# Three edits in a two-layer kernel: norm sums on ScalarE, the first chunk's delta on VectorE, all result rows fetched at once

## The chip, the cores and the metric

The kernel runs on one core of a Trainium2 chip. A core has a tensor engine for matmuls (PE, with its weight loads shown as PEld), a vector engine (DVE, VectorE), an activation engine (ACT, ScalarE), a general engine (POOL, GpSimd), and a sync engine (SP) that here only issues transfers. Each engine works through its own list of instructions in order; an instruction can wait on semaphores for another engine or for a transfer (DMA). SBUF is the on-chip memory with 128 partitions, PSUM the memory that matmuls write to.

The metric is the device time in microseconds (us) of one execution; less is better. The profile is of one further execution, and its own time is given beside the median of the runs.

## The reference

The input is x, 64 sequences of 64 tokens with 256 features (4096 tokens), and a condition for each sequence. Two layers each add an attention-like part and a feed-forward part to x:

```python
x = x + attn0(cond_scan0(x, cond))          # softmax attention over a conditioned scan
x = x + ffn0(modulated(x, cond))            # the 1.58-bit feed-forward below
x = x + mamba(rnn(x, cond))                 # selective scan over a tanh recurrence
x = x + moe_ffn(mixture(x, cond))           # two mixtures of experts, top 2 of 8 each
```

The parts that the change touches, cut to their core:

```python
def bitlinear(x, norm_w, w):                # ffn0: w1 (1024 x 256), then w2 (256 x 1024)
    v = mean(x**2, axis=-1)
    x_norm = x * rsqrt(v + 1e-8) * norm_w
    scale = 127 / clip(max(abs(x_norm)), 1e-5)
    x_q = clip(round(x_norm * scale), -128, 127) / scale
    return x_q @ ternary(w).T
h = bitlinear(x, n1, w1); h = act_scale * relu(h)**2 + act_bias; y = bitlinear(h, n2, w2)

delta = softplus(delta_lr @ W_dt + b_dt)    # mamba, 512 inner features, 16 states
dA = exp(delta[..., None] * A); dBx = delta[..., None] * B * xc[..., None]
h = dA_t * h + dBx_t; y = sum_n(h * C_t) + D * x_t          # along each sequence

x = x + sum over a token's 2 chosen experts of  weight * expert(x)      # the last step
```

## The kernel before

Activations are held with features on the partitions: 256 features are two blocks (KD = 2) of 128, and the 4096 tokens are worked in 8 chunks of 512 (NCH = 8, CH = 512). The program is written in a framework that takes tiles from pools, sets the semaphores, and orders each engine's instructions itself from what depends on what; where a written line lands in an engine's list therefore depends on its neighbours too. The stages follow each other: conditioned scan and attention (to about 377 us of the profile), ffn0 with the recurrence of layer 1 beside it (to about 656), mamba with the shared experts of the mixture beside it (to about 1895), the routed experts of the mixture, the experts of the last feed-forward (to about 2745), and the last rows.

**ffn0.** Tokens are worked in 16 pairs of 128 rows. Each of 23 turns runs nine stages, each on a different pair, so that seven pairs are in flight; from the eighth turn on the turns also issue four steps of the recurrence (L820 on PE, L829 on ACT). In each turn:

- ACT squares and sums the rows of one pair's first input (L596 on gm, 256 features) and of another pair's hidden layer (L596 on h, 1024 features), into a small tile `ss`.
- `roots_of` turns both sums into 1/sqrt(mean + eps): L605 on DVE makes mean + eps for each of the two, L608 on DVE a first guess from the bits, and L610 to L620 on POOL eleven small operations of refinement.
- `weighted` multiplies by the norm's weights and takes the largest magnitude: for gm with L632 on POOL, for h with L634 on DVE; L635 on DVE is the maximum.
- `rounded` makes the scale (L643, L644 on DVE, L645, L646 on POOL; L644 reads what L620 wrote) and rounds (L651 on ACT for h, L653 on DVE for gm, L655 on DVE for both).
- The rest are products, with L660 on POOL for the scaled input, L669, L697 and L725 on DVE, and L695, L712, L721 on ACT.

**mamba.** Each chunk has two halves (PI = 2 of the NI = 4 blocks of 128 inner features) of 16 states: 32 steps a chunk, 256 in all. `head` makes a chunk's convolution, its delta and delta times x. Its last lines for each half make softplus by L963 to L969 on ACT and L967 on DVE and end with three operations of 128x1024 elements on POOL:

```python
nc.gpsimd.tensor_add(z, z, t2)      # L970
nc.gpsimd.tensor_sub(z, z, u)       # L971
nc.gpsimd.tensor_mul(u, z, v.xc[:, i0 : i0 + PI, :])    # L972
```

Chunk 0's head runs whole ahead of the loop; the others are spread over the steps of the chunk before. A step has L1045 on POOL (input, two steps ahead, into one of five `hb` buffers), L1052 on ACT (decay, one step ahead), L1084 on DVE (two scans), L1086 on DVE (times C, spread by PE at L997), and L1100 on PE (sum of states). The scans and products of all steps are kept in order by an order token.

**Last rows.** The last experts scatter their weighted rows to DRAM (`ffn_y`, two rows a token), by L1352 on POOL. x, stored in DRAM as x_mid by the mamba stage, is loaded in eight pieces of 512 KB by L2010, between the last expert tiles of the feed-forward; expert weights (L1537) and gathered rows (L1345) are loaded through the same SP queue. For each chunk, `routing.fetch` (L1361) then brings 1024 KB of rows into one of two buffers, PE transposes the blocks of 128x128 and adds a token's two results in PSUM (L2022, 16 matmuls a chunk), DVE adds x (L2031), and SP sends 256 KB for each k (L2032). The buffers come from the same pool `px` as the pieces of x.

Of the kernel before, what the change touches and what calls it, by code (L numbers as in the profile page):

```python
# [13 lines left out]
F32 = mybir.dt.float32  # L14
BF16 = mybir.dt.bfloat16
I32 = mybir.dt.int32
AF = mybir.ActivationFunctionType
ALU = mybir.AluOpType
# [3 lines left out]
P = 128  # L22
B, L, D = 64, 64, 256
NT = B * L
CH = 512
NCH = NT // CH
KD = D // P
# [10 lines left out]
def setup(ctx, tc, a):  # L38

    nc = tc.nc  # L40
    g = SimpleNamespace(nc=nc, tc=tc, a=a)
    const = ctx.enter_context(tc.tile_pool(name="const", bufs=1))
    g.ident = const.tile([P, P], F32, name="ident")
    make_identity(nc, g.ident)
    g.identb = const.tile([P, P], BF16, name="identb")
    make_identity(nc, g.identb)
    g.ones = const.tile([P, 1], F32, name="one")
    nc.vector.memset(g.ones, 1.0)
    g.magic = const.tile([P, 1], F32, name="magic")
    nc.vector.memset(g.magic, MAGIC)  # L50
    g.eps = const.tile([P, 2], F32, name="eps")
    nc.vector.memset(g.eps, EPS)
    g.guess = const.tile([P, 4], F32, name="guess")
    nc.vector.memset(g.guess, 1597463007.0)
    g.condT = const.tile([P, KD, B], F32, name="condT")
    nc.sync.dma_start(g.condT, a["condT"].rearrange("(k p) b -> p k b", p=P))
    g.x = tc.dram_tile((D, NT), F32, name="x_mid").rearrange("(k p) t -> p k t", p=P)
    return g
# [24 lines left out]
def bank(g, shape=(P, CH), dt=F32, tag="ps"):  # L83
    tag = g.tag or tag
    return g.psum.tile(list(shape), dt, tag=tag, name=tag)
# [485 lines left out]
def ffn0(g, w, steps, loads):  # L571
# [5 lines left out]
    nc, tc = g.nc, g.tc  # L577
# [7 lines left out]
    with (  # L585
# [12 lines left out]
        def roots_of(turn_, which):  # L598


            st = roots[turn_] = p3.tile([P, 4, 2, T], F32, name="roots")
            v, r, y, u = (st[:, i, which, :] for i in range(4))
            ss = sums.pop(turn_)
            for i, n in ((0, D), (1, F))[which]:
                nc.vector.scalar_tensor_tensor(st[:, 0, i, :], ss[:, i, :], 1.0 / n, g.eps, ALU.mult, ALU.add)  # L605
            flat = lambda t: t.rearrange("p i t -> p (i t)")
            first = g.guess[:, : flat(v).shape[1]]
            nc.vector.scalar_tensor_tensor(flat(r).bitcast(I32), flat(v).bitcast(I32), -0.5, first, ALU.mult, ALU.add)  # L608
            gp = nc.gpsimd
            gp.tensor_mul(y, r, r)  # L610
            gp.tensor_mul(y, y, v)
            gp.tensor_scalar(u, y, 0.375, -1.25, ALU.mult, ALU.add)
            gp.tensor_mul(u, u, y)
            gp.tensor_scalar(u, u, 1.875, None, ALU.add)
            gp.tensor_mul(r, r, u)
            gp.tensor_mul(y, r, r)
            gp.tensor_mul(y, y, v)
            gp.tensor_scalar(y, y, -0.5, 1.5, ALU.mult, ALU.add)
            gp.tensor_mul(r, r, y)
            gp.tensor_scalar(u, r, 127.0 / 1e-5, None, ALU.mult)  # L620
# [109 lines left out]
        for turn_ in range(NP + depth):  # L730
# [6 lines left out]
            for i, (stage, late) in enumerate(stages):  # L737
                if i % 2 == 0:
                    next(more, None)
                p = turn_ - late  # L740
# [120 lines left out]
def mamba(g, w, hs, beside):  # L861
# [3 lines left out]
    nc, tc = g.nc, g.tc  # L865
# [5 lines left out]
    PI = 2  # L871
# [6 lines left out]
    with (  # L878
# [17 lines left out]
        rows = 2 * 32 + S  # L896
# [12 lines left out]
        def head(c, v):  # L909

            tok = ts(c, CH)
            v.xc = p2.tile([P, NI, CH], F32, name="xc")
            v.delta, v.dx, v.sz = [], [], []
            v.dbc = p2.tile([W, CH], F32, name="dbc")
            v.parts = parts[c % 2]
            for i in range(NI):
                ps = one()
                for k in range(KD):
                    nc.tensor.matmul(ps, w.Win[:, k, ts(i, P)], hs2[:, k, tok], start=(k == 0), stop=(k == KD - 1))  # L919
                    if k == 0:  # L920
                        yield MID
                acc = v.xc[:, i, :]
                nc.scalar.activation(acc, ps, AF.Identity, bias=w.col[:, 0, i : i + 1], scale=w.taps[:, i, 3:4])
                for s in range(1, 4):
                    to = seq(acc)[:, :, s:]
                    nc.vector.scalar_tensor_tensor(  # L926
                        to, seq(ps)[:, :, : L - s], w.taps[:, i, 3 - s : 4 - s], to, ALU.mult, ALU.add
                    )
                yield
            nc.scalar.activation(v.xc, v.xc, AF.Silu)  # L930
            yield
            ps = one()
            for i in range(NI):
                nc.tensor.matmul(ps[:W, :], w.Wxp[:, i, :], v.xc[:, i, :], start=(i == 0), stop=(i == NI - 1))
                if i < NI - 1:
                    yield MID
            nc.scalar.copy(v.dbc, ps[:W, :])

            v.B = tc.dram_tile((S, CH), F32, name=f"B{c}")
            nc.sync.dma_start(v.B, v.dbc[R : R + S, :])  # L940


            r = slice(C0, W)
            nc.scalar.copy(v.parts[32 : 32 + S, :], ps[r, :])
            nc.vector.tensor_sub(ps[r, :], ps[r, :], v.parts[32 : 32 + S, :])
            nc.scalar.copy(v.parts[0:S, :], ps[r, :])
            nc.vector.tensor_sub(v.parts[64 : 64 + S, :], ps[r, :], v.parts[0:S, :])
            yield


            for i0 in range(0, NI, PI):
                z, u = (p3.tile([P, PI, CH], F32, name=n) for n in ("delta", "dx"))
                v.delta.append(z)
                v.dx.append(u)
                t2 = p1.tile([P, PI, CH], F32, name="t2")
                for i in range(PI):
                    ps = one()
                    nc.tensor.matmul(ps, w.Wdt[:, ts(i0 + i, P)], v.dbc[:R, :], start=True, stop=True)
                    nc.scalar.activation(z[:, i, :], ps, AF.Relu, bias=w.col[:, 1, i0 + i : i0 + i + 1])
                    nc.scalar.activation(u[:, i, :], ps, AF.Abs, bias=w.col[:, 1, i0 + i : i0 + i + 1])  # L960
                    yield
                nc.scalar.activation(u, u, AF.Exp, scale=-1.0)
                nc.scalar.activation(t2, u, AF.Identity, bias=unit[:, 0:1])  # L963
                for i in range(PI):
                    ps = one()
                    nc.scalar.activation(ps, t2[:, i, :], AF.Identity, bias=unit[:, 1:2])
                    nc.vector.tensor_sub(u[:, i, :], ps, u[:, i, :])  # L967
                    yield
                nc.scalar.activation(t2, t2, AF.Ln)  # L969
                nc.gpsimd.tensor_add(z, z, t2)  # L970
                nc.gpsimd.tensor_sub(z, z, u)  # L971
                nc.gpsimd.tensor_mul(u, z, v.xc[:, i0 : i0 + PI, :])  # L972
                yield

        def gates(c, v, i0):
# [94 lines left out]
        for s in range(LAST):  # L1070
            c, j = divmod(s, STEPS)
            p, n = divmod(j, S)
# [25 lines left out]
            for i in range(PI):  # L1098
                for t in range(CH // P):
# [4 lines left out]
                        start=(n == 0 and t == 0),  # L1104
                        stop=(n == S - 1 and t == CH // P - 1),
                        is_transpose=True,
                        skip_group_check=True,
# [8 lines left out]
            while left < (j + 1) * LEFT // (STEPS - AHEAD):  # L1116
                left += 1
                got = next(pieces, None) if mid else next(urgent, END)
                if got is END:
                    got = next(pieces, None)  # L1120
# [12 lines left out]
TT = CH // P  # L1133
# [777 lines left out]
def mixtures(g, mix, x, weights, out, last, work, close):  # L1911
# [6 lines left out]
    nc, tc = g.nc, g.tc  # L1918
# [13 lines left out]
    with ExitStack() as ctx:  # L1932
# [5 lines left out]
        n = moe0.ntl  # L1938
# [67 lines left out]
        xs = []  # L2006
# [3 lines left out]
            nc.sync.dma_start(x, g.x[:, :, ts(c, CH)])  # L2010
            xs.append(x)
        some(tiles2, None)
        for c in range(NCH):
            rows = px.tile([P, TT, 2, D], F32, name=f"rows3_{c % 2}")
            routing.fetch(c, rows)
            x = xs[c]
            for k in range(KD):
                po = bank(g, tag="acc")

                for t in range(TT):  # L2020
                    for j in range(2):
                        nc.tensor.matmul(  # L2022
                            po[:, ts(t, P)],
                            rows[:, t, j, ts(k, P)],
                            g.ident,
                            start=(t == 0 and j == 0),
                            stop=(t == TT - 1 and j == 1),
                            is_transpose=True,
                            skip_group_check=True,
                        )  # L2030
                nc.vector.tensor_add(x[:, k, :], x[:, k, :], po)  # L2031
                nc.sync.dma_start(out[ts(k, P), ts(c, CH)], x[:, k, :])  # L2032
        close_px()


def scoped(tc, name, side=None, bufs=1):

    stack = ExitStack()
    kw = {"side": side} if side else {}
    return stack.enter_context(tc.tile_pool(name=name, bufs=bufs, **kw)), stack.close  # L2040
# [148 lines left out]
```

## Time and profile before

| | |
|---|---|
| median of 3 runs | 2802.39 us (2801.14 to 2802.47) |
| profiled execution | 2796.62 us, of which span 2794.9 us |
| mean granted PE clock | 0.924 |
| PE busy | 2350.0 us (84%) |
| DVE busy | 1787.2 us (64%) |
| ACT busy | 1381.1 us (49%) |
| POOL busy | 1327.4 us (47%) |
| ffn0, 467 to 583 us | DVE 112.38, PE 104.78, ACT 95.81, POOL 69.79 busy of 116.00 |
| last rows, 2747 to 2792 us | PE 24.15, DVE 11.01 busy of 45.00 |

Busy time is that of an engine's instructions, without the waits between them; an instruction that is held while it runs[...] counts as busy. The operations at issue, by line:

| line, engine | shape | times | mean ns |
|---|---|---|---|
| L605 DVE, 467 to 583 us | 128x2 | 17 | 705 |
| L970, L971, L972 POOL, 690 to 726 us | 128x1024 | 2 each | 2349, 2350, 2355 |
| L1045 POOL | 128x1024 | 256 | 2358 |
| L1086 DVE | 128x1024 | 256 | 1219 |
| L2022 PE, last rows | 128x128 f32 | 128 | 370 |
| L2031 DVE, last rows | 128x512 | 16 | 688 |

The transfers of 2700 to 2796 us, from the view of DMA issues (size of each, median from issue to landing):

```profile
rows<-ffn_y SPq DMA_DIRECT2D x8, 1024.0 KB, 6.1
out_dram<-x SPq DMA_DIRECT2D x16, 256.0 KB, 4.1
```

### The profile page before, as it was taken

To read this page: it belongs to the slowest core of one execution; us is meant where nothing else is said; L and a number is where in the kernel's file an instruction comes from. 1 tells how busy PE (TensorE), PEld (TensorE's weight loads), DVE (VectorE), ACT (ScalarE), POOL (GpSimd) and SP (SyncE) were. 2 spreads that over 40 slices of the span, in tenths; PEclk is the share of its full clock that TensorE was granted. 3 is DMA by queue.
4 is the path that set the end of the run, shared out by engine and by line. 5 is a ranking of instruction groups with operands and counts; after the bars stand their busy time and mean duration, and the time that the engine had idled before them with its cause. 6 is when DMAs were issued, how large, how long until landed. Compare 5 with 4: busy or idle time off the path is not lost.

```text
span 2794.9 us, 34560 instructions
## 1 busy us (share of the span) xinstructions
PE 2350.0 (84%) x12060; PEld 1692.7 (61%) x12060; DVE 1787.2 (64%) x3028; ACT 1381.1 (49%) x2278; POOL 1327.4 (47%) x1158
## 2 busy tenths in 40 slices
PE   3979966996668888887788888779987999999996
PEld 3634435774345555555555555557765778888885
DVE  0577648982899798888979888883354443323332
ACT  0567527884565758576566757443332222222220
POOL 0022336540786777777577868754647341111110
PEclk9989988997769899998889899999999999999997
DMA  9999920002112121212112121315777757555555
GB/s 224 372 358 346 283 70 1 1 1 91 63 66 83 57 79 65 74 63 79 46 65 95 57 95 65 117 35 167 250 259 260 294 188 266 200 200 200 197 191 186
DMA packets 180630, 406.05 MB, mean 145 GB/s; under 512 B 24913, under 2 KB 84562, under 8 KB 175074
## 3 DMA queue, kind: packets, MB, share of 16 engines
q1 hardware_dynamic: 167010, 366.80, 38.7%
q0 software_dynamic: 13440, 36.98, 3.4%
q8 instruction: 97, 1.59, 0.2%
q14 instruction: 83, 0.68, 0.1%
HBM read 280.76 MB, written 144.98 MB: 152 GB/s over the span
## 4 chain that ended last, share of the span: by engine, by line
PE 46%; DVE 26%; issue 7%; ACT 6%; POOL 5%; DMA 4%; SPq 0%; DVEq 0%; POOLq 0%; ACTq 0%
DVE hb L1084 12%; PE ps L1678 11%; PE acc L1576 8%; PE out L450 4%; DVE hb L1086 3%; PE mq L1814 2%; PE yp L1100 2%; PE ps L1645 2%; PE mq L1830 2%; PE mp L981 2%; DVE xc L926 1%; POOL hb L1045 1%; DVE h L634 1%; PE mp L919 1%; PE s L416 1%
## 5 line engine op out<-in xcount | busy, mean ns | idle before, releaser
L1045 POOL TENSOR_TENSOR hb<-dx,Bn 128x1024 f32<-128x1024 f32 x256 | 601.4, 2358 | 261.9 <-PE yp L1100 257.3
L1084 DVE TENSOR_TENSOR_SCAN hb<-dA,hb 128x512 f32<-128x512 f32 x512 | 602.6, 1208 | 33.3 <-ACT dA L1052 30.8
L1052 ACT ACTIVATE dA<-delta,negA 128x504 f32<-128x504 f32 x512 | 344.3, 683 | 308.2 <-DVE hb L1084 305.0
L1100 PEld LDWEIGHTS yp<-ident,hb 128*128 128x128 f32 x2048 | 269.6, 153 | 183.0 <-issue 145.5
L1086 DVE TENSOR_TENSOR hb<-hb,cb 128x1024 f32<-128x1024 f32 x256 | 312.0, 1219 | 82.6 <-PE cb L997 65.2
L1678 PE MATMUL ps<-gxT,w 128*128 128x256 f32 (+1 forms) x1600 | 324.1, 361 | 0.8 <-DVE gxT L1553 0.8
L1678 PEld LDWEIGHTS ps<-gxT,w 128*128 128x128 f32 x1600 | 276.3, 190 | 46.3 <-issue 12.4
L1100 PE MATMUL yp<-ident,hb 128*128 128x128 f32 x2048 | 303.9, 293 | 0.0
L1814 PE MATMUL mq<-x,moe_s 128*128 128x256 f32 x896 | 255.7, 419 | 48.3 <-ACT up L1821 26.9
L1352 POOL DMA_INDIRECT ffn_y<-gy,to x72 | 69.4, 964 | 428.8 <-ACT gy L1578 416.3
L1814 PEld LDWEIGHTS mq<-x,moe_s 128*128 128x128 f32 x896 | 172.1, 208 | 116.0 <-ACT up L1821 35.8
L1682 DVE TENSOR_TENSOR gh<-gs,ps 128x256 f32<-128x256 f32 (+1 forms) x200 | 78.7, 393 | 207.3 <-ACT gs L1681 207.3
L997 PE MATMUL cb<-parts,pick 80*128 80x512 bf16 x256 | 106.1, 415 | 113.5 <-DVE hb L1086 98.3
L1576 PE MATMUL acc<-w,gh 128*128 128x256 f32 (+1 forms) x864 | 188.6, 388 | 0.0
L1681 ACT ACTIVATE gs<-ps 128x256 f32<-128x256 f32 (+1 forms) x200 | 72.6, 363 | 230.0 <-PE ps L1678 223.2
L1578 ACT ACTIVATE gy<-acc,wt 128x256 f32<-128x256 f32 x152 | 67.1, 473 | 234.8 <-PE acc L1576 222.3
L1576 PEld LDWEIGHTS acc<-w,gh 128*128 128x128 f32 (+1 forms) x864 | 145.8, 190 | 30.3 <-issue 13.1
L432 POOL TENSOR_TENSOR E<-E,z 128x1024 f32<-128x1024 f32 x32 | 61.6, 1926 | 193.7 <-DVE z L431 109.9
L1830 PE MATMUL mq<-moe_s,sh 128*128 128x256 f32 x448 | 116.8, 400 | 6.6 <-ACT up L1821 6.6
L450 PE MATMUL out<-oT,hs 128*128 128x512 f32 x256 | 119.4, 611 | 1.5 <-ACT oT L443 1.5
L1352 POOL DMA_INDIRECT moe_y<-gy,to x80 | 77.7, 971 | 71.7 <-ACT gy L1578 53.8
L1830 PEld LDWEIGHTS mq<-moe_s,sh 128*128 128x128 f32 x448 | 84.0, 197 | 42.5 <-issue 20.3
(465 smaller groups left out, 4363.8 us busy)
## 6 DMA issues: line engine op xcount, KB each, us to landing
w<-ffn_w SPq DMA_DIRECT2D x40, 2176.0 KB, 9.1
Bn<-B SPq DMA_DIRECT2D x128, 512.0 KB, 3.7
moe_x<-fill SPq DMA_DIRECT2D x130, 260.0 KB, 5.9
ffn_x<-fill SPq DMA_DIRECT2D x129, 260.0 KB, 6.0
w<-moe_w SPq DMA_DIRECT2D x48, 512.0 KB, 4.8
ffn_w<-in_ffn_W_dram SPq DMA_DIRECT2D x16, 640.0 KB, 8.4
gx<-moe_x SPq DMA_DIRECT2D x32, 260.0 KB, 5.0
gx<-ffn_x SPq DMA_DIRECT2D x32, 260.0 KB, 9.5
```

The lines of the kernel that those rows point to most:

```text
L450: nc.tensor.matmul(ps, M[:, o, ts(k, P)], v.o[:, o], start=(o == 0), stop=(o == H // 2 - 1))
L997: nc.tensor.matmul(t, pick[:, n : n + 1].to_broadcast([rows, P]), v.parts, start=True, stop=True)
L1045: nc.gpsimd.tensor_mul(hb, vs[c].dx[p], Bn[:, n % NB, :].unsqueeze(1).to_broadcast([P, PI, CH]))
L1052: nc.scalar.activation(decays[s][i][:, :, 1:], seq(vs[c].delta[p][:, i, :])[:, :, 1:], AF.Exp, scale=A[:, p * PI + i, n : n + 1],)
L1084: ins = nc.vector.tensor_tensor_scan(h, dA[i].rearrange("p b l -> p (b l)"), h, 0.0, ALU.mult, ALU.add)
L1086: ins = nc.vector.tensor_tensor(hb, hb, cb.unsqueeze(1).to_broadcast([P, PI, CH]), ALU.mult)
L1100: nc.tensor.matmul(yp[i][:, t, :], hb[:, i, ts(t, P)], g.ident, start=(n == 0 and t == 0), stop=(n == S - 1 and t == CH // P - 1), is_tran ...
L1352: i = self.g.nc.gpsimd.indirect_dma_start(out=self.y, out_offset=bass.IndirectOffsetOnAxis(ap=to, axis=0), in_=y, in_offset=None)
L1576: nc.tensor.matmul(po[s], h, w, start=(i == 0), stop=(i == n - 1))
L1678: nc.tensor.matmul(ps[:, j, :], v.w12[:, k, ts(j * (full + 1) + i, P)], v.xT[:, k, :], start=(k == 0), stop=(k == KD - 1))
L1814: nc.tensor.matmul(ps[:, i % 2, :], w[:, k, ts(i, P)], xu[:, k, :], start=(k == 0), stop=(k == KD - 1))
L1830: nc.tensor.matmul(ps[:, t, :], h[:, i, ts(t, P)], self.s2[:, i, :], start=(i == 0), stop=(i == NS - 1))
```

## The change

There are three edits.

1. In `roots_of`, mean + eps is made by an activation on ACT (Identity, with scale 1/n and the column eps as bias) in place of the operation on DVE; the tile eps shrinks to one column.
2. In `head`, the three last operations of each half run on DVE for chunk 0 and on POOL, as before, for the others.
3. For the last rows, a pool of its own, opened after the expert pools are closed, holds eight row buffers. All eight fetches are issued ahead of the loop over chunks. In the loop, DVE adds a token's two rows (128x1024), PE transposes the sum (8 transposes a chunk), DVE adds x for each k, and one transfer of 512 KB sends the chunk.

```diff
-    g.eps = const.tile([P, 2], F32, name="eps")
+    g.eps = const.tile([P, 1], F32, name="eps")
...
             for i, n in ((0, D), (1, F))[which]:
-                nc.vector.scalar_tensor_tensor(st[:, 0, i, :], ss[:, i, :], 1.0 / n, g.eps, ALU.mult, ALU.add)
+                nc.scalar.activation(st[:, 0, i, :], ss[:, i, :], AF.Identity, bias=g.eps, scale=1.0 / n)
...
                 nc.scalar.activation(t2, t2, AF.Ln)
-                nc.gpsimd.tensor_add(z, z, t2)
-                nc.gpsimd.tensor_sub(z, z, u)
-                nc.gpsimd.tensor_mul(u, z, v.xc[:, i0 : i0 + PI, :])
+                e = nc.gpsimd if c else nc.vector
+                e.tensor_add(z, z, t2)
+                e.tensor_sub(z, z, u)
+                e.tensor_mul(u, z, v.xc[:, i0 : i0 + PI, :])
                 yield
...
         some(tiles2, None)
-        for c in range(NCH):
-            rows = px.tile([P, TT, 2, D], F32, name=f"rows3_{c % 2}")
-            routing.fetch(c, rows)
-            x = xs[c]
-            for k in range(KD):
-                po = bank(g, tag="acc")
-                for t in range(TT):
-                    for j in range(2):
-                        nc.tensor.matmul(
-                            po[:, ts(t, P)],
-                            rows[:, t, j, ts(k, P)],
-                            g.ident,
-                            start=(t == 0 and j == 0),
-                            stop=(t == TT - 1 and j == 1),
-                            is_transpose=True,
-                            skip_group_check=True,
-                        )
-                nc.vector.tensor_add(x[:, k, :], x[:, k, :], po)
-                nc.sync.dma_start(out[ts(k, P), ts(c, CH)], x[:, k, :])
-        close_px()
+    pl, close_pl = scoped(tc, "rows")
+    rows = [pl.tile([P, TT, 2, D], F32, name=f"rows3_{c}") for c in range(NCH)]
+    for c in range(NCH):
+        routing.fetch(c, rows[c])
+    for c in range(NCH):
+        x, got = xs[c], rows[c]
+        nc.vector.tensor_add(got[:, :, 0, :], got[:, :, 0, :], got[:, :, 1, :])
+        for k in range(KD):
+            po = bank(g, tag="acc")
+            for t in range(TT):
+                nc.tensor.transpose(po[:, ts(t, P)], got[:, t, 0, ts(k, P)], g.ident)
+            nc.vector.tensor_add(x[:, k, :], x[:, k, :], po)
+        nc.sync.dma_start(out.rearrange("(k p) t -> p k t", p=P)[:, :, ts(c, CH)], x)
+    close_pl()
+    close_px()
```

## The prediction

> **What bounds the kernel now.** The diff touches three stages, so the page's totals come second. I read the page's chain first, then that chain cut to two stretches, then one line, two timelines and one table of windows. The page's chain by engine:
>
> ```profile
> PE 46%; DVE 26%; issue 7%; ACT 6%; POOL 5%; DMA 4%; SPq 0%; DVEq 0%; POOLq 0%; ACTq 0%
> ```
>
> PE carries nearly half, mostly in stages that the change leaves alone. What counts is who carries the three places.
>
> Place one, the first feed-forward stage (about 377 to 656 us). The windows give for 467 to 583 us DVE 112.38 busy of 116.00, PE 104.78, ACT 95.81: DVE is the bound. The moved operation, by its line, then in DVE's and POOL's timelines (start, duration, engine):
>
> ```profile
> L605 DVE SCALAR_TENSOR_TENSOR roots<-ss,eps x32: 142/158/1484, 383.9 to 618.8; 128x2 f32<-128x2 f32 x32
> ```
> ```profile
> 525.52 1.48 DVE L605 SCALAR_TENSOR_TENSOR roots<-ss,eps 128x2 f32<-128x2 f32 x1
> 526.92 3.44 DVE L634 SCALAR_TENSOR_TENSOR h<-h,act,n 128x2048 f32<-128x2048 f32 x1
> ```
> ```profile
> 525.29 1.69 POOL L660 TENSOR_TENSOR xs<-xT,ys 128x512 f32<-128x512 f32 x1
> 526.95 1.27 POOL L632 TENSOR_TENSOR gm<-gm,n 128x512 f32<-128x512 f32 x1
> ```
>
> L605 takes 0.15 us in its median and up to 1.48, on the same two elements. At 525.52 it ends with POOL's L660 (526.98), and L634 behind it takes 3.44 instead of its usual 2.3, ending POOL's L632 first. So the long ones wait for POOL; about 15 of the 32 do.
>
> Place two, the start of the mamba stage, in the chain of waits (start, duration, who):
>
> ```profile
> 695.06 2.35 POOL delta L970
> 697.48 2.35 POOL delta L971
> 699.91 2.37 POOL dx L972
> 702.34 2.36 POOL hb L1045
> 704.72 2.35 DVE hb L1084 x2
> ```
>
> Three POOL operations stand in series before the first scan, while DVE idles: 7.07 us of chain.
>
> Place three, the last 48 us, in the same view and then in windows (PE, PEld, DVE, ACT, POOL busy; clock, DMA share, GB/s):
>
> ```profile
> 2747.14 5.75 DMA rows<-ffn_y
> ...
> 2760.27 7.22 DMA rows<-ffn_y
> ...
> 2771.31 5.89 DMA rows<-ffn_y
> ...
> 2780.97 7.99 DMA rows<-ffn_y
> ```
> ```profile
> 2752.00:2757.00 5.00, 3.98 (x19) 4.01 (x20) 0.99 (x2) 0.00 (x0) 0.00 (x0) 0.50 0.61 229
> 2757.00:2762.00 5.00, 2.09 (x15) 1.85 (x13) 1.76 (x3) 0.00 (x0) 0.00 (x0) 0.84 0.84 231
> 2762.00:2767.00 5.00, 3.65 (x16) 3.27 (x16) 1.06 (x2) 0.00 (x0) 0.00 (x0) 0.50 1.04 399
> 2787.00:2792.00 5.00, 3.75 (x25) 3.17 (x23) 2.75 (x4) 0.00 (x0) 0.00 (x0) 0.84 0.39 147
> ```
>
> Transfer, transposes, add and next transfer take turns, because two row buffers serve eight chunks. The DMA engines reach 399 GB/s in one window and stand at 147 to 231 in others.
>
> **What the Trainium skill says.** "SBUF — State Buffer", section "Who interferes with whom": a VectorE instruction that reads two SBUF operands and a GpSimd instruction that reads SBUF exclude each other for their whole length, while tensor_reduce doesn't contend. The trace agrees: L605 at 525.52 above, and L616 on POOL takes 1.24 at 520.88, beside DVE's L697, instead of 0.20. "ScalarE: Activation LUTs", section "Table sets: the hidden batching unit": the plain functions are in every table set. No run here shows it yet for this place; in the order of ACT's instructions both kernels load tables 122 times. Its section "What ACT_TABLE_LOAD costs" prices an ACTIVATE with a column bias at about 0.28 us plus 0.83 ns an element, and I price the moved ones by that; the trace has 0.385 us for L829 with 128 elements, which fits. "DMA: Bandwidth & Descriptors", section "Specifications", puts HBM at about 358 GB/s a core; the 399 above is more, so the measurement decides.
>
> **Part 1, mean square plus eps from DVE to ACT.** DVE loses 32 instructions. 17 of them are short: 17 x 0.15 = 2.6 us. The other 15 take 1.04 to 1.48; were their waits to vanish, 15 x 1.2 = 18 us more would go. They don't all vanish: where L634 (two SBUF operands) stands behind L605, as at 526.92, L634 will wait for the same POOL instruction. Where the reduction L635 stands behind, about 9 times, it can start.
>
> Against that, the order of DVE's instructions changes: in a steady turn it becomes L669, L655 (gm), L634, L635, L655 (h), L608, L635 (gm), L697, L725, L643, L644, L653. Between L608 and L644 there are then 3.3 us of DVE work (0.67+1.2+1.2+0.2), while POOL's chain L610 to L620 takes 11 x 0.285 = 3.1 plus about 1.1 of waiting for L697: L644 would wait about 1.1. Queued behind it on DVE are L653, L697 and the next turn's products; ACT waits for those. L655 (gm) may also meet L660: 0.9. A turn from L634 to L634 now takes 14.48 in the mean of 467 to 583. DVE's own work in it is about 11.8 (1.13+0.1+0.6+2.4+1.21+0.2+0.2+0.6+0.6+0.34+2.26+2.2), PE's about 12.4; 11.8 + 1.1 + 0.9 + some locks (0.1 to 0.7) gives 13.9 to 14.5. So 0 to 0.5 us a turn over 11 turns: I take 0.27, **-3 us**.
>
> ACT takes two L605 a turn behind the pair L651: 2 x 0.28 = 0.56 us; L829 of the recurrence is behind them, and ACT has 20 of 116 us free. Without that cover, in the last two turns (605 to 620 us, ACT busy 14.19 of 15), one L605 costs 0.28 each, which is in the range. Ends: -16 (all long waits go, the order costs nothing) and +6 (the two waits cost half a us a turn more than what goes).
>
> **Part 2, the first chunk's three adds on DVE.** A 128x1024 two-operand instruction takes 1.13 to 1.22 on DVE (L1086) and 2.35 on POOL. First half: 3 x 2.35 falls to 3 x 1.17, -3.5 us on the chain. The second half's three also move, and in DVE's order they now stand among the first step's scans and products; before, POOL did them at 711 to 721 and nobody waited. That adds 3 x 1.17 = 3.5 of DVE work there, plus waits of 0.25, 0.75 and 1.15 against POOL's back-to-back L1045 (2.36 each): 5.6. POOL in turn is freed of 7. ACT's order moves the first step's second L1052 behind L969 and a table load, to about 704.9 us; it is then due at about 704 and costs one us. Before, a stall of 1.51 at 720.24 (DVE waits for ACT's dA) falls away in the later start. Walking the steps by hand, the fifth ends at 725.1 instead of 724.2: **+1 us**. Ends: -3.5 (second half hidden) and +4 (each add meets a full L1045).
>
> **Part 3, the tail.** All eight fetches can be issued at 2747.1: the last scatter lands at 2747.05 and the space is free by then. A chunk needs on DVE one 128x1024 add (1.2) and two L2031 (0.69): 2.6; on PE 8 transposes in place of 16 (at most 1.9); on the DMA engines 1.05 MB, 2.6 at 399 GB/s. The reads keep the engines full, and writes queue behind them on SP. Bytes stay 8.39 MB in and 4.19 out. I allow 3.3 us until 2750.4 with 0.5 MB moved (the present start, by the GB/s of the DMA view's slices), then 7.9 MB at 395 = 20.0: 2770.4. The writes run at 377 GB/s, the rate at which the DMA view shows x_mid<-xT written at 646 to 658: 11.1, so 2781.5, plus 0.5 to land and 1.1 to the end as now: 2783.1 against 2794.9. The last chunk's compute (1.2+1.9+1.4) lies under earlier chunks' writes; without that cover it would add 4. **-11.5 us**; ends -8 (rates 10% lower) and -13.
>
> The row buffers no longer share a pool with x, so SP's order puts the first x loads (L2010) before the expert weights of 2272.21. x waits for the last send, about 2276, and the weights and rows behind it slip by some 6 us: to about 2290, while PE wants them at 2296.9. Cost nothing; a few us if that slack is gone.
>
> **Sum**: -3 + 1 - 11.5 = -13.5, on the profiled 2796.62 (span 2794.9 and 1.7 around it): 2783.1. The median of the runs stands 5.8 higher, 2802.39: so **2789**.
>
> **Rivals.**
> - A: the long L605 simply vanish. For it: nine are followed by a reduction. Against: the new wait at L644. Part 1 gives -16, the sum -26.5: 2776.
> - B: the tail moves less. Reads and writes meet in one queue and the rate sags to 330 GB/s with another 2 us at start: -4.5, the sum -6.5: 2796. Against: 399 and 384 in windows that hold reads and writes together.
> - C: the gain is given back: part 1 at +6 and part 2 at +4, so -1.5: 2801, not to be told from before.
> - D, slower: in the feed-forward stage L644 waits for POOL's chain, which L697 locks out. With 1.1 there, 0.9 at L655 and the old locks merely moved, a turn is 16.5 and 11 turns cost +22; with +1 - 11.5 that is +11.5: 2814. It decides from 1.0 us a turn on. For it: POOL's L616 and L617 already show 1.24 and 1.12. Against: 9 stalls of 1.2 over those turns must go first.
>
> That the edit doesn't do what it says is unlikely: the order shows the moves on each engine.
>
> **How the numbers follow.** 0.2%, some 5.6 us, is what a measurement can tell from no change. Forecast 0.55, A 0.17, B 0.09, C 0.11, D 0.08. Forecast, A and B are faster: 0.81; C is the same: 0.11; D is slower: 0.08. The range goes from 2776 (A) to 2800 (near C): it leaves out D, part of C and what lies beyond A, about 0.2.
>
> **What would show it.** Right: rows<-ffn_y issued eight times within a few us after 2747, windows near 395 GB/s until 2770, the end 11 to 12 us after its old distance; first scan 3.5 us earlier from the stage's start and the fifth step later by about one; no L605 on DVE, and L644 idle for POOL's L620. Wrong: turns below 13.5 us (A) or above 15.5 (D), DMA windows under 350 (B), PE waiting for w near 2297.

## The result and the profile after

The changed kernel takes 2782.81 us (median of 6 runs, 2777.95 to 2787.55) against 2801.76 us before (6 runs, 2797.84 to 2803.09). The ratio is 0.9935, 95% interval 0.9922 to 0.9948: 19 us less, between 15 and 22. The profiled execution took 2777.95 us with a span of 2776.0 us, at a mean PE clock of 0.927.

First the page of the changed kernel, its chain by engine:

```profile
PE 45%; DVE 23%; ACT 9%; issue 8%; POOL 5%; DMA 3%; SPq 0%; DVEq 0%; ACTq 0%; POOLq 0%
```

DVE's share of the chain fell from 26 to 23%, ACT's rose from 6 to 9%. The shares don't say what was gained where; that takes a look at each place. From edit 2's added line on, line numbers are one higher than before.

**ffn0.** The moved operation, then a stretch of DVE's and of POOL's timeline (start, duration, engine, line, in brackets the idle time before it and who ended it):

```profile
L605 ACT ACTIVATE roots<-ss,eps x32: 279/284/296, 383.6 to 616.8; 128x2 f32<-128x2 f32 x32
```
```profile
512.63 0.15 DVE L608 SCALAR_TENSOR_TENSOR roots<-roots,guess 128x4 int32<-128x4 int32 x1
...
516.98 0.23 DVE L644 SCALAR_TENSOR_TENSOR st<-st,roots 128x2 f32<-128x2 f32 x2 [1.05 <-POOL roots L620]
...
519.62 1.15 DVE L655 TENSOR_SCALAR q<-gm 128x512 bf16<-128x512 f32 x1
520.69 2.34 DVE L634 SCALAR_TENSOR_TENSOR h<-h,act,n 128x2048 f32<-128x2048 f32 x1
```
```profile
513.43 1.19 POOL L612 TENSOR_SCALAR roots<-roots 128x4 f32<-128x4 f32 x1
...
516.71 0.23 POOL L620 TENSOR_SCALAR roots<-roots 128x4 f32<-128x4 f32 x1
...
518.39 2.10 POOL L660 TENSOR_TENSOR xs<-xT,ys 128x512 f32<-128x512 f32 x1 [0.34 <-PE ps L667]
```

On ACT all 32 take 0.28 us; none waits. Two new waits stand on DVE in the steady turns: 1.05 us at L644, because POOL's chain from L610 to L620 lost a microsecond at L612 beside L697, and L655 takes 1.15 where it took 0.4, beside L660 (until 547 us; from 561 on it takes 0.41 again). L634 is 2.34 in these turns; in two of the first four it took 3.60 and 3.35. A turn is 13.77 us (506.92 to 520.69) where the mean before was 14.48.

What went and what came stands in the view by lines for 467 to 583 us, first of the kernel before, then of the changed one (after the bar: busy us and mean ns of one, then the idle time before it):

```profile
L605 DVE SCALAR_TENSOR_TENSOR roots<-ss,eps 128x2 f32<-128x2 f32 x17 | 12.0, 705 | 0.0
L644 DVE SCALAR_TENSOR_TENSOR st<-st,roots 128x2 f32<-128x2 f32 x16 | 6.0, 404 | 0.8 <-POOL roots L620 0.8
L634 DVE SCALAR_TENSOR_TENSOR h<-h,act,n 128x2048 f32<-128x2048 f32 x8 | 20.9, 2618 | 0.0
L655 DVE TENSOR_SCALAR q<-gm 128x512 bf16<-128x512 f32 x9 | 3.8, 426 | 0.2
```
```profile
L644 DVE SCALAR_TENSOR_TENSOR st<-st,roots 128x2 f32<-128x2 f32 x16 | 1.9, 158 | 8.1 <-POOL roots L620 8.1
L634 DVE SCALAR_TENSOR_TENSOR h<-h,act,n 128x2048 f32<-128x2048 f32 x9 | 21.1, 2343 | 1.6 <-ACT junk L596 1.6
L655 DVE TENSOR_SCALAR q<-gm 128x512 bf16<-128x512 f32 x8 | 7.7, 960 | 0.0
```

Not only L605's 12.0 us are gone from DVE: L644 itself, which took up to 1.32 us beside POOL's L660, is short too, and L634 no longer takes 3.44. That is more than the waits at L644 and the longer L655 cost.

**Start of mamba.** DVE's timeline:

```profile
692.37 1.23 DVE L971 TENSOR_TENSOR delta<-delta,t 128x1024 f32<-128x1024 f32 x1 [2.28 <-ACT t L969]
693.63 1.23 DVE L972 TENSOR_TENSOR delta<-delta,dx 128x1024 f32<-128x1024 f32 x1
694.89 1.23 DVE L973 TENSOR_TENSOR dx<-delta,xc 128x1024 f32<-128x1024 f32 x1
...
698.64 1.22 DVE L1085 TENSOR_TENSOR_SCAN hb<-dA,hb 128x512 f32<-128x512 f32 x1 [0.69 <-POOL hb L1046]
700.23 1.77 DVE L971 TENSOR_TENSOR delta<-delta,t 128x1024 f32<-128x1024 f32 x1 [0.37 <-ACT t L969]
702.23 1.22 DVE L1085 TENSOR_TENSOR_SCAN hb<-dA,hb 128x512 f32<-128x512 f32 x1 [0.23 <-ACT dA L1053]
703.37 1.92 DVE L972 TENSOR_TENSOR delta<-delta,dx 128x1024 f32<-128x1024 f32 x1
705.21 1.21 DVE L1087 TENSOR_TENSOR hb<-hb,cb 128x1024 f32<-128x1024 f32 x1
706.34 2.25 DVE L973 TENSOR_TENSOR dx<-delta,xc 128x1024 f32<-128x1024 f32 x1
```

The first half's three additions take 1.23 each and the first scan starts 6.3 us after the end of the first L969 (692.34); before it was 9.8 (694.93 to 704.72). The second half's three stand among the first step's scans and take 1.77, 1.92 and 2.25 beside POOL's multiplications.

**Last rows.** SP's issue of the fetches, DVE's and PE's timelines, then windows (PE, PEld, DVE, ACT, POOL busy; clock, DMA share, GB/s):

```profile
2736.05 13.08 SPq L1362 DMA_DIRECT2D rows<-ffn_y  x8
```
```profile
2748.62 1.22 DVE L2020 TENSOR_TENSOR rows<-rows 128x1024 f32<-128x1024 f32 x1
2751.06 0.69 DVE L2025 TENSOR_TENSOR x<-x,acc 128x512 f32<-128x512 f32 x1 [1.23 <-PE acc L2024]
2751.92 0.69 DVE L2025 TENSOR_TENSOR x<-x,acc 128x512 f32<-128x512 f32 x1 [0.17 <-PE acc L2024]
2752.52 1.22 DVE L2020 TENSOR_TENSOR rows<-rows 128x1024 f32<-128x1024 f32 x1
```
```profile
2749.94 1.94 PE L2024 MATMUL acc<-ident,rows 128*128 128x128 f32 x8 [1.96 <-issue]
2753.84 1.94 PE L2024 MATMUL acc<-ident,rows 128*128 128x128 f32 x8 [1.96 <-issue]
```
```profile
2755.00:2760.00 5.00, 2.72 (x12) 1.94 (x10) 3.45 (x5) 0.00 (x0) 0.00 (x0) 0.50 1.04 387
...
2765.00:2770.00 5.00, 2.50 (x11) 2.15 (x12) 2.95 (x4) 0.00 (x0) 0.00 (x0) 0.50 0.74 284
2770.00:2775.00 5.00, 1.38 (x7) 0.98 (x5) 1.38 (x2) 0.00 (x0) 0.00 (x0) 0.50 0.38 143
```

A chunk takes 3.90 us (2749.94 to 2753.84). PE works for 1.94 of it and stands for 1.96 (the view names no releaser here, but it starts at 2753.84, 0.1 after the row addition has ended); DVE waits 1.23 for PE. The DMA engines are full until about 2765 and then run dry. From the last scatter's landing (2735.6) to the end it takes 40.4 us, against 47.8 before.

Whole times of one kernel scatter by 10 us and more here, so the experiments are read by three marks in the profile, which hardly depend on what came before: the end of the recurrence beside ffn0 (end of the last L829, on which mamba starts), the time from the end of the first L969 to the end of the fifth product of mamba, and the tail from the last scatter's landing to the end of the span. All in us; the ratio is that of the medians of whole runs to the kernel before, with its interval.

| kernel | recurrence ends | to the fifth product | tail | ratio |
|---|---|---|---|---|
| before, and again | 656.0, 660.8 | 29.36, 29.37 | 47.8, 48.8 | 1 |
| changed, and again | 653.9, 652.7 | 30.97, 30.97 | 40.4, 40.6 | 0.9935 (0.9922 to 0.9948), 0.9938 (0.9922 to 0.9953) |
| edit 1 alone | 650.8 | 29.12 | 51.6 | 0.9961 (0.9946 to 0.9977) |
| edit 2 alone | 658.8 | 30.97 | 48.7 | 0.9977 (0.9961 to 0.9994) |
| edit 3 alone | 660.3 | 29.36 | 40.4 | 0.9971 (0.9957 to 0.9986) |
| changed without edit 2 | 652.8 | 29.03 | 40.5 | 0.9930 (0.9917 to 0.9944) |
| rows added on POOL | 650.8 | 30.96 | 36.6 | 0.9917 (0.9900 to 0.9935) |
| rows added on PE | 650.4 | 30.96 | 37.7 | 0.9924 (0.9909 to 0.9938) |
| half of edit 2, rows on POOL | 650.2 | 27.19 | 36.8 | 0.9907 (0.9894 to 0.9921) |
| L605 with one operand, on DVE | 659.7 | 29.36 | 51.2 | 0.9987 (0.9975 to 0.9999) |

### The profile page after: what moved, and what is told of

It is laid out like the page before. It is cut to its first block, busy times and chain, and to the rows that moved or that the text cites. A ratio compares the mean times of both kernels' runs of the same rounds, so it can differ in the third digit from the quotient of the medians.

```text
span 2776.0 us, 34424 instructions
## 1 busy us (share of the span) xinstructions
PE 2337.2 (84%) x11977; PEld 1677.6 (60%) x11996; DVE 1794.8 (65%) x3010; ACT 1383.6 (50%) x2310; POOL 1304.1 (47%) x1152
## 4 chain that ended last, share of the span: by engine, by line
PE 45%; DVE 23%; ACT 9%; issue 8%; POOL 5%; DMA 3%; SPq 0%; DVEq 0%; ACTq 0%; POOLq 0%
DVE hb L1085 13%; PE ps L1679 10%; PE acc L1577 8%; PE out L450 4%; DVE hb L1087 3%; PE yp L1101 2%; PE mq L1815 2%; PE ps L1646 2%; PE mq L1831 2%; DVE xc L926 2%; PE mp L982 2%; POOL hb L1046 1%; PE s L416 1%; PE acc L441 1%; PE ps L1687 1%
## 5 line engine op out<-in xcount | busy, mean ns | idle before, releaser
L1053 ACT ACTIVATE dA<-delta,negA 128x504 f32<-128x504 f32 x512 | 344.6, 683 | 316.8 <-DVE hb L1085 315.4
```

The source lines that it names most:

```text
L1053: nc.scalar.activation(decays[s][i][:, :, 1:], seq(vs[c].delta[p][:, i, :])[:, :, 1:], AF.Exp, scale=A[:, p * PI + i, n : n + 1],)
```

## The experiments

**Each edit alone.** The kernel before, with only the lines of one edit.

Edit 1 alone:

```diff
-                nc.vector.scalar_tensor_tensor(st[:, 0, i, :], ss[:, i, :], 1.0 / n, g.eps, ALU.mult, ALU.add)
+                nc.scalar.activation(st[:, 0, i, :], ss[:, i, :], AF.Identity, bias=g.eps, scale=1.0 / n)
```

> Edit 1 alone on the kernel before. In the changed kernel's profile the ffn0 stage ends 5.3 us earlier (first x_mid<-xT at 640.9 instead of 646.2) with turns of 13.6 to 13.8 us instead of 14.5. Theory 'each edit acts in its own stage': this kernel is 5 us faster than before, ffn0 ends at about 641, mamba lasts as long as before. My prediction's term was 3 us. Rival 'the later stages gain too': the whole is 8 to 13 us faster, because the 8 us that mamba's later chunks and the experts gained in the profile belong to a shift that begins here.

Its runs have a median of 2787.14 us against 2797.97, 11 us less (6 to 15 by the interval). The recurrence ends at 650.8. Over all profiles the five without edit 1 end it at 656.0 to 660.8 (mean 659.1), the seven with it at 650.2 to 653.9 (mean 651.7): edit 1 is worth 7.5 us, and the first theory's 5 was too low because the first profile of before lay at the early end. The 11 us lie in the rival's range, but 7.5 lies in the same interval, so whole times don't decide. In its profile the later stages show no gain: from the first chunk's write of x_mid to the last scatter's landing it takes 1875.2 us, where the twelve profiles lie between 1865.3 and 1882.2. The rival isn't needed.

Edit 2 alone:

```diff
-                nc.gpsimd.tensor_add(z, z, t2)
...
+                e = nc.gpsimd if c else nc.vector
+                e.tensor_add(z, z, t2)
```

> Edit 2 alone on the kernel before. In the changed kernel's profile the fifth step of mamba ends 1.0 us earlier than before, while the stage started 5.4 us earlier: edit 2 would cost 4.4 us at the start of mamba (the prediction said 1), of which the first chunk's end still shows 2.8. Theory 'a loss at the start that stays': 1 to 4 us slower than before. Rival 'the start is absorbed': no difference. Rival 'the later chunks run better because of it': 3 or more us faster.

The median is 2790.42 us, 7.5 less than before, which speaks for the third reading; the marks do not. In each of the five profiles with edit 2 as written the fifth product comes 30.96 to 30.97 us after the first L969, in each of the six without it 29.03 to 29.37: 1.6 us lost (1.9 where edit 1 is in), not 4.4. The 4.4 counted from the end of ffn0's own writes, but mamba waits for the recurrence. From the fifth product to the first chunk's end (its write of x_mid) it then takes 139.8 to 140.7 us with the edit and 141.0 to 142.0 without, so that some 1.1 comes back; what gives it back wasn't tried.

Edit 3 alone has the lines of the last rows from the change.

> Edit 3 alone on the kernel before. From the last scatter's landing to the end the changed kernel took 40.4 us instead of 47.8. Theory 'tail alone': 7.5 us faster than before, the stages up to 2740 us as before. Prediction's term: 11.5 faster. Rival 'earlier loads of x move the experts too': 10 to 11 us faster, with the last scatter 3 us earlier.

The median is 2790.52 us, also 7.5 less. Its tail is 40.4 us. The tails without edit 3 are 47.8, 48.7, 48.8, 51.2 and 51.6 (mean 49.6), the four with it as written 40.4 to 40.6: 9.2 us. Why the old tail takes 47.8 in one profile and 51.6 in another wasn't settled. The experts are not moved: from mamba's last write of x_mid to the last scatter's landing it takes 849.7 to 854.7 us with the earlier loads of x and 848.6 to 853.1 without.

By their medians the three edits alone add up to 26 us, more than the 19 of all together. Each of the three has an interval of some 4 us to either side, so this is no contradiction, but it is why the terms are taken from the marks.

**The rows added on POOL.**

```diff
-        nc.vector.tensor_add(got[:, :, 0, :], got[:, :, 0, :], got[:, :, 1, :])
+        nc.gpsimd.tensor_add(got[:, :, 0, :], got[:, :, 0, :], got[:, :, 1, :])
```

> The changed kernel with the addition of a token's two rows on POOL instead of DVE. Theory 'round trip': in the changed kernel a chunk takes 3.90 us because DVE's row addition (1.22) waits behind the two x additions, PE's transposes wait for it, and the x additions for PE; with POOL's own queue (2.36 a chunk) the transfers set the pace at 2.6 a chunk: the tail takes 36 to 37 us instead of 40.4, 3.5 to 4.5 us faster than the changed kernel. Rival 'transfers already set the end': no faster, 40 us.

The tail falls to 36.6 us. POOL's timeline, and a window of this kernel:

```profile
2755.91 2.36 POOL L2020 TENSOR_TENSOR rows<-rows 128x1024 f32<-128x1024 f32 x1 [0.38 <-DMA rows<-ffn_y]
2758.61 2.35 POOL L2020 TENSOR_TENSOR rows<-rows 128x1024 f32<-128x1024 f32 x1 [0.35 <-DMA rows<-ffn_y]
```
```profile
2770.00:2775.00 5.00, 3.09 (x14) 2.29 (x12) 2.75 (x4) 0.00 (x0) 1.77 (x1) 0.50 1.06 409
```

Now each addition waits for its rows, 2.70 us apart, and the DMA engines stay full to the last 5 us: transfers set the pace. The theory of the round trip (the loop in which DVE and PE wait for each other) holds, and its rival falls.

**The changed kernel again**, beside the next three.

> The changed kernel once more, to stand beside the next three on one chip. Theory 'sum of places': the recurrence of the ffn0 stage ends at 651 to 654 us (before 656 to 660), from the end of the first L969 to the fifth product of mamba 30.97 us (before 29.36), tail 40.4 us (before 48 to 52). About 0.9935 of before.

It is the same within what runs scatter: 2779.33 us, ratio 0.9938, with the three marks where they were expected.

**Edit 2 undone** in the changed kernel; POOL makes all the additions again.

> The changed kernel with edit 2 undone. Theory 'edit 2 costs at the start': from the end of the first L969 to the fifth product 29.2 to 29.4 us instead of 30.97, and 0 to 2 us faster than the changed kernel in all, within what runs scatter. Rival 'edit 2 helps the later chunks' (edit 2 alone ran 0.23% faster than before): 4 to 8 us slower than the changed kernel, with mamba from its fifth step to its end 4 us longer.

The median is 2779.33 us, the same as the changed kernel's, and 29.03 us to the fifth product. So edit 2 does nothing that whole times show, and the 0.23% that it seemed to bring alone isn't borne out. From the first chunk's end to the last scatter's landing, where nothing differs but the earlier loads of x of edit 3, the twelve profiles take 1865.3 to 1882.2 us; the profile of edit 2 alone is the lowest of them. That the 0.23% was such scatter is argued, not shown.

**The rows added on PE**, as before the change, with all fetches at once:

```diff
-        nc.vector.tensor_add(got[:, :, 0, :], got[:, :, 0, :], got[:, :, 1, :])
...
-                nc.tensor.transpose(po[:, ts(t, P)], got[:, t, 0, ts(k, P)], g.ident)
+                for j in range(2):
+                    nc.tensor.matmul(
+                        po[:, ts(t, P)],
+                        got[:, t, j, ts(k, P)],
...
```

> The changed kernel without the row addition on DVE: all eight fetches at once, but PE adds the two results again (16 transposes a chunk). Theory 'round trip': without the addition PE need not wait for DVE; 16 transposes of 0.21 to 0.24 us are 3.4 to 3.9 us a chunk at the half clock and 2.0 at full clock, so the tail takes 36 to 40 us against 40.4: the addition on DVE bought nothing or cost up to 4 us, and the gain of edit 3 is the fetches'. Rival 'the addition bought the gain': tail 44 us or more.

The tail is 37.7 us, 2.8 less than with the addition on DVE. PE's timeline:

```profile
2753.48 1.94 PE L2024 MATMUL acc<-ident,rows 128*128 128x128 f32 x16 [0.78 <-DVE x L2033]
2756.19 1.94 PE L2024 MATMUL acc<-ident,rows 128*128 128x128 f32 x16 [0.77 <-DVE x L2033]
2760.02 1.94 PE L2024 MATMUL acc<-ident,rows 128*128 128x128 f32 x16 [1.89 <-DMA rows<-ffn_y]
```

Sixteen transposes here take the 1.94 us that eight took in the changed kernel. The granted clock is the reason, in the third column from the right of two windows of this kernel:

```profile
2739.00:2744.00 5.00, 4.21 (x26) 4.24 (x27) 1.37 (x2) 0.00 (x0) 0.00 (x0) 0.62 1.01 387
2744.00:2749.00 5.00, 3.80 (x34) 3.38 (x33) 2.76 (x4) 0.00 (x0) 0.00 (x0) 1.00 1.04 388
```

During the first 32 transposes, which run without a pause (5.13 us, two chunks), the granted clock rises to full and stays there until the transposes are done, while it stayed at 0.50 through the changed kernel's whole tail; that the unbroken work is what raises it wasn't tried. The gain of edit 3 doesn't need the addition on DVE. It is that of the fetches, or of the single send for each chunk, which came with them and was not tried apart. The addition halves PE's count of transposes, but the eight take as long as the sixteen do here, and the loop with DVE gives 2.8 us back.

**Half of edit 2, and the rows on POOL:**

```diff
-                e = nc.gpsimd if c else nc.vector
+                e = nc.gpsimd if c or i0 else nc.vector
```

> The changed kernel with the rows added on POOL and with only the first half of chunk 0's delta on DVE. Theory 'the second half costs': without the second half's three additions among the first scans, the time from the end of the first L969 to the fifth product is 26.8 to 28.3 us instead of 30.97 (before 29.36); with the tail at 36.6 the kernel is 6 to 8 us faster than the changed one. Rival 'ACT's order costs, not the additions': 30 to 31 us, 4 us faster.

2772.52 us, ratio 0.9907: the lowest of all (its interval overlaps those with the rows added on POOL and on PE), and 6.8 us below the changed kernel's median beside it. To the fifth product it takes 27.19 us, 3.8 less than with both halves on DVE and about 2 less than with none. What stands in DVE's way at the start is now ACT's second decay:

```profile
696.78 1.22 DVE L1085 TENSOR_TENSOR_SCAN hb<-dA,hb 128x512 f32<-128x512 f32 x1 [0.70 <-POOL hb L1046]
700.36 1.22 DVE L1085 TENSOR_TENSOR_SCAN hb<-dA,hb 128x512 f32<-128x512 f32 x1 [2.36 <-ACT dA L1053]
```

So the second half's additions were the loss: the order of ACT, with the second L1053 behind a table load, stayed as it was.

**L605 on DVE with one operand**, in the kernel before:

```diff
-                nc.vector.scalar_tensor_tensor(st[:, 0, i, :], ss[:, i, :], 1.0 / n, g.eps, ALU.mult, ALU.add)
+                nc.vector.tensor_scalar(st[:, 0, i, :], ss[:, i, :], 1.0 / n, EPS, ALU.mult, ALU.add)
```

> The kernel before with L605 left on DVE, but as a tensor_scalar with the number eps in place of the tile, so that it reads one SBUF operand. Theory 'two operands lock': the long L605 (up to 1.48 us) fall to 0.15 us throughout, and turns shorten where no L634 follows; the ffn0 stage ends 1 to 5 us earlier. Rival 'any DVE instruction in this place waits for POOL's', also one with a single operand: durations of 1.0 to 1.5 us stay in some of the 32, and the stage ends when it did (recurrence's end at 656 to 660 us).

The view of this line in that kernel (durations in ns: least, median, most):

```profile
L605 DVE TENSOR_SCALAR roots<-ss x32: 148/170/1489, 384.2 to 620.9; 128x2 f32<-128x2 f32 x32
```

Nothing changed in the stage: the longest is 1489 ns (1484 before), and the recurrence ends at 659.7. Each of the 15 long ones ends within 0.03 us of the end of an L660 or L632 on POOL. Whole times are 0.13% lower, with an interval that barely leaves out 1 (0.9975 to 0.9999); no mark says where. The theory of two operands falls, the rival holds: as a tensor_scalar the operation waits for POOL too. The Trainium skill, "SBUF — State Buffer", section "Who interferes with whom", has both halves of it: tensor_scalar is among the operations that can take the port pair which VectorE shares with GpSimd, and ACT never waits on anyone. The trace agrees, with 1.49 us here and 0.28 on ACT.

**The kernel before again**, for a second profile.

> The kernel before once more, for a second profile of it: what scatters between executions of the same code. Theory 'scatter': recurrence's end at 656 to 660 us, 29.36 us to the fifth product, a tail of 48 to 52 us, and from the first chunk's end to the last scatter's landing 1865 to 1882 us, the spread that nine kernels with the same code there have shown.

Its span is 2798.3 us. The fifth product (29.37), the tail (48.8) and the middle (1879.3 us) fall in their ranges; the recurrence ends at 660.8, 0.8 later than expected.

## Why the prediction was right, and which terms were off

The forecast was 2789 us, with -3, +1 and -11.5; measured is 2782.81. The three terms by the marks are -7.5, +1.6 (of which some 1.1 returns in the same chunk) and -9.2, a sum of -15 to -16, inside the interval of -15 to -22. What the medians show beyond the marks, 3 to 4 us, has no place that an edit touches. That the total came out near is in part luck: part 1 brought 4.5 us more than forecast and part 3 2.3 less, so the two misses half cancel, and 2782.81 lies almost as near to rival A's 2776 as to 2789.

**Part 1, mis-sized.** The two waits came about as priced: 1.05 at L644 (about 1.1 said), and 0.7 more at L655 (0.9 said). The term that was off is "some locks (0.1 to 0.7)", the stretches in which DVE and POOL hold each other up: 11.8 + 1.05 + 0.7 leaves 0.2 of 13.77 for them, near the low end, because in the steady turns of the new order L634 no longer met a POOL instruction, and because L644's own long executions went, which the prediction hadn't counted. That makes 0.71 a turn instead of the 0.27 taken.

That 11 such turns would be 7.8, close to the 7.5 measured, is luck. By the starts of L634, in the mean of the seven profiles with edit 1 against the five without, the lead is 4.9 us at the fifth turn, 10.6 at the twelfth and 6.8 at the last. The seven steady turns gain 0.8 each, the first ones, for which the prediction had no term, bring 4.9, and the last four give 3.8 back. In the last ones ACT is the busiest engine (11.36 of 12.13 us in the turn from 588.87), so part of this may be the moved operation's 0.28 each, as the prediction said; no run shows it. How much of the gain is the locks and how much the new order of DVE's instructions was not tried apart.

The reason given for the long L605, two SBUF operands, was too narrow: with one it waited as long. ACT's cost was as said, 0.28 us each, and no table load came with it (121 in the trace before and after, none of them in ffn0). L829, which the prediction held against the price of a column bias, names no such column in the kernel; the moved operation itself bears the price out.

**Part 2, right.** The first scan came 3.5 us earlier, as said. The second half's additions took 0.54, 0.69 and 1.02 more than 1.23, or 2.25 in all (0.25 + 0.75 + 1.15 = 2.15 said). The fifth product was 1.6 late, against 0.9 by the walk. What the prediction did not ask is whether the second half had to move at all: leaving it on POOL gave 27.19 instead of 30.97.

**Part 3, a step that failed.** The prediction set DVE's 2.6 us, PE's 1.9 and the transfer's 2.6 a chunk beside each other, let the transfers set the pace, and took the compute to lie under them (without that cover it would add 4, it said). But DVE's instructions of one chunk stand on both sides of PE's: the row addition of the next chunk is behind the two x additions, these wait for PE, and PE waits for the row addition. So a chunk takes 1.22 of addition, 1.2 until the first half is transposed, and two x additions with what lies between them, 3.9 together. 2783.1 - 2747.1 = 36.0 was forecast for the tail, 40.4 came, 4.4 more. The tail before, 47.8 in the profile used, has a mean of 49.6 over five, so that the gain is 9.2 rather than 7.4; against the profile that it started from, the forecast was 4 off and not 2.3. With the round trip taken away the tail is 36.6: the transfer sum itself was right. The eight fetches were issued over 13 us and not within a few, as its signs had it; that cost nothing the sum would show. Nor did the x loads that moved ahead of the weights, as said.

**Rivals.** D's wait at L644 was there at its price but did not outweigh the locks that went. A is half true: more of the stalls went than was taken, but the new waits ate the rest. B's low rates did not come while the DMA engines were full: 387 GB/s and more. The 284 and 143 of the last windows stand where the loop left them dry. C's giving back stayed at 0.5 to 1.6 us.

## What to carry to other kernels

When engines pass a chunk to and fro, the pace isn't the busiest engine's sum but the length of the loop through the in-order queues: list who waits for whom across two neighbouring chunks before taking a maximum, and put one leg on an engine that has no other leg. The tiny operation that took ten times its median in some executions was waiting, each time until an instruction of POOL ended; fewer operands didn't help, another engine (ACT) did. Then look at what becomes late next, here a chain on POOL. Moving an operation off a slow engine pays only on the path: the first half of edit 2 gained, the second half, for which nobody waited, cost more than that.

## What the runs showed of the hardware

A VectorE tensor_scalar of 128x2 elements with one SBUF operand took up to 1.49 us beside GpSimd, as much as the two-operand form. With half as many transposes a chunk PE was granted half the clock (0.50 against 1.00), and 8 took the same 1.94 us as 16. From the first chunk's end to the last scatter's landing code that is the same but for the place of the x loads took between 1865.3 and 1882.2 us in twelve profiles, a scatter nearly as large as the whole change is worth; the time to the fifth product agreed to 0.02 us in the five profiles with edit 2 as written.
